# A transformer block on one core: value loads on ACT's queue, broadcasts of reciprocals on GpSimd's, first conditioning rows taken out of PSUM by ACT, and turned chunks in wide tiles

## The chip, the cores and the metric

The kernel runs on one core of a Trainium2 chip. The metric is device time in microseconds, the median over runs. A core has five engines with a queue of instructions each: PE (TensorE, matmuls into PSUM), DVE (VectorE), ACT (ScalarE), POOL (GpSimd) and SP (SyncE, which only issues transfers). Each queue is worked off in order: an instruction that waits for a semaphore holds up all behind it on its engine. A transfer (DMA) is an instruction of the queue that issues it (SP, ACT or POOL). All numbers are float32.

## The reference

One conditioned transformer block, for `x` of 2 x 2048 x 576, 16 heads of 36 channels, a hidden width of 2304:

```python
ada = silu(c) @ W_ada + b_ada                  # one row of 6 x 576 per batch entry
shift_msa, scale_msa, gate_msa, shift_mlp, scale_mlp, gate_mlp = split(ada, 6)
h = layernorm(x) * (1 + scale_msa) + shift_msa
q, k, v = heads(h @ W_qkv + b_qkv)
attn = softmax(einsum('blhd,bmhd->bhlm', q * 36 ** -0.5, k))
x = x + gate_msa * (einsum('bhlm,bmhd->blhd', attn, v) @ W_proj + b_proj)
h = layernorm(x) * (1 + scale_mlp) + shift_mlp
x = x + gate_mlp * (gelu(h @ W_fc1 + b_fc1) @ W_fc2 + b_fc2)
```

The layer norm has no parameters of its own; `gelu` is the tanh form.

## The kernel before

Every instruction of note goes through `seq` and keeps the order in which the program states it. So the order on each engine is the order of the Python code, and the tile framework adds the waits.

**The start (the `front` pools, L174 to L582).** Tokens are worked in stages of 512 (`queries_keys_values`, L207), a generator that is advanced step by step: load x; means, variances and the normed tile `xn` (DVE); turn `xn` into `hT`, channels on partitions, in five chunks of 128 channels (`turn`, L233: four transposes on PE into one PSUM bank; `modulated`, L151: scale and shift on the way out of PSUM, even chunks on DVE, odd ones on ACT); then the projections `pq` (L277) for queries and keys, and `pv` (L327) for values, which are stored to memory (`qk_d`, `v_d`). Five stages run here: the four of the first batch entry and the first of the second. PSUM has three wide tiles of two banks (`wide`, tag "w") and two single banks (`bank`, tag "b"). The first stage turns two chunks in banks, two in a wide tile and the fifth in half of another; the other stages turn all five in the two banks, one after the other. While stage n runs its projections, the next one is turned at its seventh step (L579).

Conditioning: `rows_of` (L403) multiplies the activated condition with one sixth of `W_ada` into a wide tile `pa`; DVE copies the row out. `modulation` (L423) turns this row into columns with ten small matmuls (L431), and `done` stores them in `mod`, from which `modulated` reads. Parts 0 and 1 are made before the first `hT`. The biases of queries, keys and the first MLP matrix come in as rows `b_in` and are transposed after that (L562), in a single bank. The remaining four parts are made by `later` between the steps of the stages, with the gated copies of `W_proj` and `W_fc2`.

**Attention (L587 on).** A unit is one head of one block of 512 queries; 8 blocks of 16 heads make 128 units, each of four slots (`NG`). The loop at L1320 goes through the slots; scores run eight slots ahead of their use (`AHEAD`). In each slot: scores (`scores`, L636, 16 matmul instructions, into two wide PSUM tiles), ACT copies them to SBUF (`keep`, L649), DVE keeps a running maximum (`maxima`, L654), subtracts the final maximum (`less`, L691), ACT takes the exponential (`exps`, L695), PE multiplies by the values (`weigh`, L707). In the first slot of a unit the chain of the maximum runs for the unit ahead: PE turns the running maxima (`turn`, L672), DVE reduces them (L682), SP writes them to memory (`m_d<-mx`, L683) and reads them back on all partitions (`m<-m_d`, L686).

Loads of a unit, all on SP: keys and queries (`load_keys`, L169 and L170, called at L1326), and values (`load_values`, L617, two buffers, called at L1327 in the first slot of the unit before). A unit's result `up` has one buffer: ACT copies it (L719), DVE adds the other half (L720), and one slot later SP stores its lower half (L726, L727) and POOL adds the upper half in memory (L728, L729). The sums of the exponentials are row 0 of the result.

**Beside attention** PE gets other work: the projections of the second batch entry, and for every finished block of queries `gather` and `block`. `fill` (L1304) emits one piece of it in the even slots, `advance` (L1288) one step of a generator per slot. `lights` are pieces that turn normed tiles (`turned`, L844: four transposes, L851, into a bank of `ps_f`, and ACT's `modulated`); in odd slots that aren't forced, up to two of them are emitted ahead of the scores (L1333).

`gather(k)` (L1032) loads the sums (L1035), the block's result `oT` and x; DVE takes the reciprocal (L1050), POOL writes it to `rec_d` (L1051). Then `rec_d` is read back in five steps, one chunk of 128 channels each, spread over the 36 partitions of every head: 22 transfers per block on SP (L1063) into tiles `r` that share four buffers with the normed tiles. DVE multiplies three steps later (`LAG`, L1072). `block(k)` projects (`po`, L787), adds x, norms, and runs the MLP: `pf` (L1160) from weights loaded one pair of chunks ahead (`load_cols`, L754 and L757, on POOL), `py` (L1208) from weights loaded at L1123 (POOL), and DVE's addition (`add`, L1220). After the last slot of attention the loop at L1381 runs the rest without it.

Of the kernel before, what the change touches and what calls it, by code (L numbers as in the profile page):

```python
# [17 lines left out]
P = 128  # L18
# [4 lines left out]
def dit_block_kernel(  # L23
# [16 lines left out]
    nc = tc.nc  # L40
    B, L, C = x.shape
# [3 lines left out]
    SCALE = D ** (-0.5)  # L45

    KC = (C + P - 1) // P
# [6 lines left out]
    NF = FF // P  # L54
    C2 = C // 2
# [3 lines left out]
    def seq(ins):  # L59

        return tc.keep_in_program_order(ins)
# [23 lines left out]
    ident = const.tile([P, P], F32, name="ident")  # L85
    make_identity(nc, ident)
    qscale = const.tile([P, 1], F32, name="qscale")
# [7 lines left out]
    NQK = 2 * C // P  # L95
    bias = const.tile([P, NQK + NF], F32, name="bias")
# [77 lines left out]
    with ExitStack() as front:  # L174
# [4 lines left out]
        def wide(name):  # L179
            return ps_w.tile([P, 2, 512], F32, tag="w", name=name)  # L180

        def bank(name):
            return ps_b.tile([P, 512], F32, tag="b", name=name)
# [23 lines left out]
        def queries_keys_values(b, tb):  # L207
            mvs = lnp.tile([P, TB, nc.vector.BN_AGGR_DIM], F32, tag="mv", name=f"mv_{b}_{tb}", bufs=2)
            xts, xns = [], []
            for i in range(TB):  # L210
                xt = lnp.tile([P, C], F32, tag="xt", name=f"xt_{b}_{tb}_{i}", bufs=8)
                by = nc.sync if (b, tb) == (0, 1) else nc.scalar
# [20 lines left out]
            def turn(kc, pt=None):  # L233
                if pt is None:
                    pt = bank(f"pt_{b}_{tb}_{kc}")
                for i in range(TB):
                    seq(nc.tensor.transpose(pt[:, ts(i, P)], xns[i][:, ts(kc, P)], ident))
                return pt

            pts = []  # L240
            if (b, tb) == (0, 0):
                spare = [wide(f"pt_{i}") for i in range(2)]
                pts = [turn(kc) for kc in range(2)]
                pts += [turn(2 + n, spare[0][:, n, :]) for n in range(2)]
                pts.append(turn(4, spare[1][:, 0, :]))
                pms.extend([spare[1][:, 1, :]])
                yield
            for kc in range(KC):
                pt = pts[kc] if kc < len(pts) else turn(kc)
# [102 lines left out]
        first_keys = []  # L352
        hTs = {}
        pms = []
        stages = [queries_keys_values(0, tb) for tb in range(NQB)] + [queries_keys_values(1, 0)]

        next(stages[0])
# [42 lines left out]
            seq(nc.tensor.transpose(pt[:, ts(kc, B)], c_in[:, ts(kc, P)], ident[:B, :B]))  # L400
        cT = ap.tile([P, KC, B], F32, name="cT")
        seq(nc.vector.tensor_copy(cT.rearrange("p k b -> p (k b)"), pt[:, 0 : KC * B]))
        def rows_of(part):  # L403

            wa = was.pop(part)
            pa = pas.pop(part) if part in pas else cleared(part)
            for n in range(2):
                for kc in range(KC):
                    at = 32 * (kc % NC)
                    seq(  # L410
                        nc.tensor.matmul(
                            pa[at : at + B, n, :C2],
                            lhsT=cT[: rows(kc), kc, :],
                            rhs=wa[: rows(kc), kc, ts(n, C2)],
                            start=(kc < NC),
                            stop=(kc == KC - 1 or 0 < kc < NC),
                        )
                    )
            t = ap.tile([P, C], F32, tag="rows", name=f"rows_{part}", bufs=2)
            seq(nc.vector.tensor_copy(t.rearrange("p (n c) -> p n c", n=2), pa[:, :, :C2]))  # L420
            return t

        def modulation(part, t):  # L423

            pm = pms.pop(0) if pms else wide(f"pm_{part}")[:, 0, :]
            if part == 0:
                pms.append(pm[:, KC * B :])
            for fc in range(KC):
                m = P if fc < KC - 1 else KL
                seq(  # L430
                    nc.tensor.matmul(  # L431
                        pm[:m, ts(fc, B)], lhsT=t[:, ds(fc * P, m)], rhs=of_b, start=True, stop=True
                    )
                )
            to = 2 * (part // 3) + (1 - part % 3)
            add = 1.0 if part % 3 == 1 else 0.0
            spans = [(0, P, 0, KC - 1), (0, KL, KC - 1, KC), (64, KL, KC - 1, KC)]

            def done():
                for at, m, lo, hi in spans:  # L440
                    seq(
                        nc.vector.tensor_scalar_add(
                            mod[at : at + m, to, lo:hi, :].rearrange("p k b -> p (k b)"),
                            pm[:m, lo * B : hi * B],
                            add,
                        )
                    )

            return done
# [103 lines left out]
            modulation(4, t)()  # L553

        next(stages[0])
        ts_ = [rows_of(part) for part in range(2)]
        next(stages[0])
        for done in [modulation(part, ts_[part]) for part in range(2)]:
            done()
        pt = bank("pt_bias")  # L560
        nb = NQK + NF
        seq(nc.tensor.transpose(pt[:, 0:nb], b_in, ident[:nb, :nb]))  # L562
        nq = C // P
        seq(nc.vector.tensor_scalar_mul(bias[:, 0:nq], pt[:, 0:nq], SCALE))
        seq(nc.vector.tensor_scalar_mul(bias[:, nq : nq + 1], pt[:, nq : nq + 1], qscale))
        seq(nc.vector.tensor_copy(bias[:, nq + 1 : nb], pt[:, nq + 1 : nb]))

        for b in range(B):
            seq(nc.vector.tensor_copy(spread[b], of_b[:, b : b + 1].to_broadcast([P, P])))
        rest = later()  # L570
        next(rest)
        next(stages[0])
        for n in range(NQB):
            if n + 2 <= NQB:
                next(stages[n + 2])
# [11 lines left out]
    with ExitStack() as main_part:  # L587
# [12 lines left out]
        class Unit:  # L600
# [11 lines left out]
            def load_values(self):  # L612
                self.v = np_.tile([P, L // P * HA + 64 - HA], F32, tag="v", name=f"v_{self.u}")
                nt = L // P * HA
                seq(nc.vector.memset(self.v[:, nt:], 0.0))
                seq(
                    nc.sync.dma_start(  # L617
                        out=self.v[:, :nt].rearrange("p (t e) -> p t e", e=HA),
                        in_=v_d[self.b].rearrange("(t p) e -> p t e", p=P)[
                            :, :, ds(self.h * HA, HA)  # L620
                        ],
                    )
                )
# [408 lines left out]
        def gather(k):  # L1032

            sums = bp.tile([P, H * QB // P], F32, tag="sums", name=f"sums_{k}")
            seq(nc.gpsimd.dma_start(out=sums, in_=flat_rows(sum_d[k])))  # L1035
            oT = hp.tile([P, KC, QB], F32, tag="big", name=f"oT_{k}")
            outs[k] = oT
            seq(
                nc.gpsimd.dma_start(
                    out=oT[:, 0 : KC - 1, :],  # L1040
                    in_=o_d[k][0 : (KC - 1) * P].rearrange("(kc p) n -> p kc n", p=P),
                )
            )
            for half in halves(oT, KC - 1):
                seq(nc.gpsimd.dma_start(out=half, in_=o_d[k][(KC - 1) * P : C]))
            b, qb = divmod(k, NQB)
            loaded[k] = load_x(f"b{k}", b, qb, gp_d[b])
            yield
            yield
            seq(nc.vector.reciprocal(sums, sums))  # L1050
            seq(nc.gpsimd.dma_start(out=flat_rows(rec_d[k]), in_=sums))  # L1051
            yield
            recs = []
            LAG = 3
            for kc in range(KC + LAG):
                if kc < KC:
                    r = xp.tile([P, CP], F32, tag="xn", name=f"r_{k}_{kc}")[:, :QB]
                    for to in (0,) if kc < KC - 1 else (0, 64):
                        f, end = kc * P, min(kc * P + P, C)
                        while f < end:  # L1060
                            n = min(D - f % D, end - f)
                            seq(
                                nc.sync.dma_start(  # L1063
                                    out=r[ds(to + f - kc * P, n), :],
                                    in_=rec_d[k][f // D, :].partition_broadcast(n),
                                )
                            )
                            f += n
                    recs.append(r)
                if kc >= LAG:  # L1070
                    c = kc - LAG
                    seq(nc.vector.tensor_mul(oT[:, c, :], oT[:, c, :], recs[c]))  # L1072
                yield
# [246 lines left out]
        for G in range(-AHEAD, NU * NG + 1):  # L1320
# [3 lines left out]
            su, sg = divmod(G + AHEAD, NG)  # L1324
            if sg == 0 and su + 1 < NU:
                units[su + 1].load_keys()  # L1326
            if g == 0 and -1 <= u and u + 1 < NU:  # L1327
                units[u + 1].load_values()
            cu, cg = divmod(G - 1 + AHEAD, NG)
            chain = cg == NG - 1 and 0 <= cu < NU  # L1330
            count(RATE)
            forced = g % 2 == 0 or G < 0 or credit > RATE
            if not forced:  # L1333
                for step in [lights.pop(0)() for _ in lights[:2]]:
                    count(-step[0])
                    step[1]()
            tiles = units[su].scores(sg) if su < NU else None
            if tiles:
                units[su].keep(sg, tiles)
            dones = fill() if forced else []  # L1340

            if 0 <= G + 1 < NU * NG:
# [98 lines left out]
```

## Time and profile before

| | us |
|---|---|
| median of 3 runs (lowest, highest) | 3733.76 (3732.9, 3734.05) |
| the profiled execution, outside | 3736.07 |
| its span, first to last instruction | 3734.3 |
| PE busy in the span | 3692.3 |
| DVE, ACT, POOL busy | 2947.2, 2329.2, 616.2 |
| mean clock granted to PE | 0.996 |

The profile is that of one execution. A line of the timeline gives start, length, engine, source line, operation, output<-inputs, shapes, count, and in brackets the idle time of the engine before it with what ended it; "SPq" is SP's queue, on which a transfer's length is the time of its issue. A line of the waits gives the engine and line that waited, for whom, the total in us, how often, and the longest. In the busy table by stretch the columns are busy us (and instructions) of PE, PE's weight loads, DVE, ACT and POOL, then PE's clock as a share of full speed, the mean busy share of the 16 DMA engines, and GB/s. A busy PE is not PE at its peak. Idle time of an engine that doesn't set the end costs nothing.

### The profile page before, as it was taken

What the parts mean: (1) busy time and instruction counts of PE and PEld (TensorE: products, weight loads), DVE (VectorE), ACT (ScalarE), POOL (GpSimd) and SP (SyncE); (2) the same over time, 40 slices, a digit from 0 to 9 for tenths busy, and PEclk for the clock granted to TensorE, in tenths of its full rate; (3) what the DMA queues carried; (4) which work ended last, traced back from release to release, by engine and by line L of the source; (5) the groups of instructions that cost most, each with busy time, mean ns of one, the idle gap of its engine ahead of it and who ended that gap; (6) DMA issues with size and microseconds to landing.
All of it is one profiled execution on the core that took longest, in us unless ns stands there. A gap on an engine that the chain in (4) does not pass through costs nothing. (4 is left out here: it accounts for less than half of the span.)

```text
span 3734.3 us, 59188 instructions
## 1 busy us (share of the span) xinstructions
PE 3692.3 (99%) x23926; PEld 1724.1 (46%) x23926; DVE 2947.2 (79%) x3002; ACT 2329.2 (62%) x2164; POOL 616.2 (17%) x868
## 2 busy tenths in 40 slices
PE   8999999999999999999999999999999999999999
PEld 4454344434444534444444444453444444444565
DVE  4627889889888898898889888988889888988422
ACT  0006777667776686677677767767667766676321
POOL 0101111211111111111121112111120211111311
PEclk9999999999999999999999999999999999999999
DMA  7733444554345343534353435424353435342522
GB/s 237 270 109 99 100 95 98 126 108 106 73 89 116 77 100 71 132 68 99 79 120 83 112 65 112 110 59 105 78 122 66 103 79 116 79 100 58 136 70 70
DMA packets 426864, 382.11 MB, mean 102 GB/s; under 512 B 313734, under 2 KB 314776, under 8 KB 426592
## 3 DMA queue, kind: packets, MB, share of 16 engines
q1 hardware_dynamic: 354336, 178.84, 22.5%
q0 software_dynamic: 69952, 194.77, 19.8%
q10 hardware_dynamic: 2304, 4.72, 0.4%
q8 instruction: 189, 3.10, 0.4%
q14 instruction: 83, 0.68, 0.1%
HBM read 306.98 MB, written 71.21 MB: 101 GB/s over the span
## 5 line engine op out<-in xcount | busy, mean ns | idle before, releaser
L649 ACT COPY e<-s 128x1024 f32<-128x1024 f32 x1024 | 989.5, 1024 | 716.2 <-PE s L636 714.4
L691 DVE TENSOR_TENSOR e<-e,m 128x2048 f32<-128x2048 f32 x512 | 1161.7, 2274 | 58.8 <-DMA m<-m_d 58.8
L654 DVE TENSOR_TENSOR acc<-acc,e 128x1024 f32<-128x1024 f32 x768 | 939.1, 1223 | 184.8 <-ACT e L649 142.7
L695 ACT ACTIVATE e<-e 128x2048 f32<-128x2048 f32 x512 | 990.9, 1936 | 20.7 <-DVE e L691 20.7
L707 PE MATMUL av<-e,v 64*64 64x512 f32 x8192 | 980.4, 594 | 0.0
L636 PE MATMUL s<-qT,kT 36*64 36x512 f32 x8192 | 974.0, 589 | 1.5 <-PE pv L327 1.0
L1208 PE MATMUL py<-w,gT 128*128 128x288 f32 x2304 | 585.6, 412 | 6.3 <-DVE x_b L1220 6.3
L636 PEld LDWEIGHTS s<-qT,kT 36*64 36x64 f32 x8192 | 311.0, 133 | 561.8 <-issue 520.6
L707 PEld LDWEIGHTS av<-e,v 64*64 64x64 f32 x8192 | 298.1, 133 | 518.9 <-issue 466.8
L1160 PE MATMUL pf<-h_b,w_b 128*128 128x512 f32 x1152 | 531.0, 604 | 0.0
L1208 PEld LDWEIGHTS py<-w,gT 128*128 128x128 f32 x2304 | 434.8, 191 | 184.8 <-issue 43.7
L728 POOL DMA_DIRECT2D o_d<-up x128 | 109.5, 856 | 2086.0 <-DMA o_d<-up 1277.4
L1160 PEld LDWEIGHTS pf<-h_b,w_b 128*128 128x128 f32 x1152 | 207.7, 189 | 318.8 <-issue 305.3
L1171 ACT ACTIVATE gT<-pf,bias 128x512 f32<-128x512 f32 x144 | 99.0, 688 | 191.3 <-PE pf L104 133.4
L682 DVE TENSOR_REDUCE mx<-mt 128x4 f32<-128x512 f32 x128 | 88.1, 688 | 159.8 <-PE mt L672 159.8
L1180 DVE SCALAR_TENSOR_TENSOR th<-th,gT 128x1024 f32<-128x1024 f32 x72 | 88.0, 1223 | 90.7 <-ACT th L1178 90.5
L654 DVE TENSOR_TENSOR acc<-e 128x1024 f32<-128x1024 f32 x128 | 155.4, 1214 | 4.4 <-ACT e L649 4.4
L1220 DVE TENSOR_TENSOR x_b<-py,x_b 128x288 f32<-128x288 f32 x192 | 81.0, 450 | 83.3 <-PE py L1208 83.2
L729 POOL DMA_DIRECT2D sum_d<-up x128 | 143.7, 1123 | 0.9 <-issue 0.9
L277 PE MATMUL pq<-hT,w_in 128*128 128x512 f32 (+1 forms) x320 | 131.8, 564 | 1.5 <-DVE hT L156 1.5
L787 PE MATMUL po<-wpr_p,oT 128*128 128x288 f32 x512 | 132.6, 412 | 0.0
L754 POOL DMA_DIRECT2D w_b<-in_L_cond_W_fc_dram x72 | 69.5, 965 | 303.1 <-PE pf L1160 272.6
(157 smaller groups left out, 2353.1 us busy)
## 6 DMA issues: line engine op xcount, KB each, us to landing
w<-w_d POOLq DMA_DIRECT2D x72, 576.0 KB, 6.0
v<-v_d SPq DMA_DIRECT2D x128, 296.0 KB
kT<-qk_d SPq DMA_DIRECT2D x256, 144.0 KB
w_b<-in_L_cond_W_fc_dram POOLq DMA_DIRECT2D x72, 512.0 KB, 4.8
m<-m_d SPq DMA_DIRECT2D x128, 256.0 KB
qT<-qk_d SPq DMA_DIRECT2D x256, 72.0 KB
w_d<-wg POOLq DMA_DIRECT2D x12, 864.0 KB, 6.8
qk_d<-ev SPq DMA_DIRECT2D x36, 256.0 KB
```

The source lines that it names most:

```text
L277: nc.tensor.matmul(pq[:, r, :n], lhsT=w_in[:, kc, cols], rhs=hT[:, kc, at], start=(kc == 0 and not (two and r)), stop=(kc == KC - 2 and tw ...
L636: nc.tensor.matmul(s[ts(c, 64), i, :], lhsT=self.kT[at, ds((2 * g + j) * P + 64 * c, 64)], rhs=self.qT[at, :], start=True, stop=True,)
L649: seq(nc.scalar.copy(self.es[g][:, j], s))
L654: top = lambda out, x, y: seq(nc.vector.tensor_max(out, x, y))
L691: seq(nc.vector.tensor_sub(e, e, m))
L695: seq(nc.scalar.activation(e, e, AF.Exp))
L707: nc.tensor.matmul(self.av[ts(i, 64), r, :], lhsT=self.v[ts(r, 64), ds((c + i * (HALF // P)) * HA, 64)], rhs=e[ts(r, 64), j, i, :], start= ...
L728: seq(nc.gpsimd.dma_start(out=o, in_=hi[1:HA, :], accum_op=ALU.add))
L729: seq(nc.gpsimd.dma_start(out=sums, in_=hi[0:1, :], accum_op=ALU.add))
L787: nc.tensor.matmul(outs[n][:, :C2], lhsT=src[:, kc, ts(i, P)], rhs=w_[:, kc, ts(n, C2)], start=(kc == 0), stop=False,)
L1160: nc.tensor.matmul(pfs[j], lhsT=wc[:, kc, ts(j, P)], rhs=h2[:, kc, :], start=(kc == 0 and j == 0), stop=(kc == KC - 2 and j == 1),)
L1208: nc.tensor.matmul(py[n][:, :C2], lhsT=gTs[f - f % 2][:, f % 2, ts(i, P)], rhs=w2s[f - f % 2][:, f % 2, ts(n, C2)], start=(j == 0), stop=( ...
```

## The change

Five edits:

1. `load_values` issues its transfer on ACT's queue instead of SP's, and is called in the second slot of the unit before, not the first.
2. The 22 broadcasts of reciprocals per block (`r<-rec_d`) are issued on POOL's queue instead of SP's.
3. In odd slots the `lights` come after the scores and their copies, not ahead of them.
4. The rows of conditioning parts 0 and 1 are copied out of PSUM by ACT. Their `modulation` matmuls are emitted before the transposes of the first stage, into the two halves of one wide tile, and are stored after them. The biases are transposed along with the first stage's fifth chunk, in the other half of its tile, and kept after the first `hT` has been made.
5. Every stage at the start turns its third and fourth chunk in a wide tile; before, the first stage alone did. The fifth chunk of the other stages stays in a single bank.

```diff
-            pts = []
-            if (b, tb) == (0, 0):
-                spare = [wide(f"pt_{i}") for i in range(2)]
-                pts = [turn(kc) for kc in range(2)]
-                pts += [turn(2 + n, spare[0][:, n, :]) for n in range(2)]
-                pts.append(turn(4, spare[1][:, 0, :]))
-                pms.extend([spare[1][:, 1, :]])
+            first = (b, tb) == (0, 0)
+            pts = [turn(kc) for kc in range(2)]
+            spare = wide(f"pt_{b}_{tb}")
+            pts += [turn(2 + n, spare[:, n, :]) for n in range(2)]
+            if first:
+                spare = wide("pt_4")
+                pts.append(turn(4, spare[:, 0, :]))
+                turn_biases(spare[:, 1, :])
                 yield
...
+        nb, nq = NQK + NF, C // P
+        turned_biases = []
+
+        def turn_biases(pt):
+            turned_biases.append(pt)
+            seq(nc.tensor.transpose(pt[:, 0:nb], b_in, ident[:nb, :nb]))
+
+        def keep_biases():
+            pt = turned_biases[0]
+            seq(nc.vector.tensor_scalar_mul(bias[:, 0:nq], pt[:, 0:nq], SCALE))
+            seq(nc.vector.tensor_scalar_mul(bias[:, nq : nq + 1], pt[:, nq : nq + 1], qscale))
+            seq(nc.vector.tensor_copy(bias[:, nq + 1 : nb], pt[:, nq + 1 : nb]))
...
-        def rows_of(part):
+        def rows_of(part, by=None):
...
-            seq(nc.vector.tensor_copy(t.rearrange("p (n c) -> p n c", n=2), pa[:, :, :C2]))
+            out = t.rearrange("p (n c) -> p n c", n=2)
+            if by is nc.scalar:
+                seq(nc.scalar.copy(out, pa[:, :, :C2]))
+            else:
+                seq(nc.vector.tensor_copy(out, pa[:, :, :C2]))
...
-            if part == 0:
-                pms.append(pm[:, KC * B :])
...
         next(stages[0])
-        ts_ = [rows_of(part) for part in range(2)]
+        ts_ = [rows_of(part, nc.scalar) for part in range(2)]
+        both = wide("pm")
+        pms.extend(both[:, n, :] for n in range(2))
+        dones = [modulation(part, ts_[part]) for part in range(2)]
         next(stages[0])
-        for done in [modulation(part, ts_[part]) for part in range(2)]:
+        for done in dones:
             done()
-        pt = bank("pt_bias")
-        nb = NQK + NF
-        seq(nc.tensor.transpose(pt[:, 0:nb], b_in, ident[:nb, :nb]))
-        nq = C // P
...
+        next(stages[0])
+        keep_biases()
         for b in range(B):
             seq(nc.vector.tensor_copy(spread[b], of_b[:, b : b + 1].to_broadcast([P, P])))
         rest = later()
         next(rest)
-        next(stages[0])
...
                 seq(
-                    nc.sync.dma_start(
+                    nc.scalar.dma_start(
                         out=self.v[:, :nt].rearrange("p (t e) -> p t e", e=HA),
...
                             seq(
-                                nc.sync.dma_start(
+                                nc.gpsimd.dma_start(
                                     out=r[ds(to + f - kc * P, n), :],
...
-            if g == 0 and -1 <= u and u + 1 < NU:
+            if g == 1 and -1 <= u and u + 1 < NU:
                 units[u + 1].load_values()
...
             forced = g % 2 == 0 or G < 0 or credit > RATE
+            tiles = units[su].scores(sg) if su < NU else None
+            if tiles:
+                units[su].keep(sg, tiles)
             if not forced:
                 for step in [lights.pop(0)() for _ in lights[:2]]:
                     count(-step[0])
                     step[1]()
-            tiles = units[su].scores(sg) if su < NU else None
-            if tiles:
-                units[su].keep(sg, tiles)
             dones = fill() if forced else []
```

More of the change, by code (lines that the diff above doesn't have):

```diff
@@ L555, in dit_block_kernel @@
         next(stages[0])
-        ts_ = [rows_of(part) for part in range(2)]
+        ts_ = [rows_of(part, nc.scalar) for part in range(2)]
+        both = wide("pm")
+        pms.extend(both[:, n, :] for n in range(2))
+        dones = [modulation(part, ts_[part]) for part in range(2)]
         next(stages[0])
-        for done in [modulation(part, ts_[part]) for part in range(2)]:
+        for done in dones:
             done()
-        pt = bank("pt_bias")
-        nb = NQK + NF
-        seq(nc.tensor.transpose(pt[:, 0:nb], b_in, ident[:nb, :nb]))
-        nq = C // P
-        seq(nc.vector.tensor_scalar_mul(bias[:, 0:nq], pt[:, 0:nq], SCALE))
-        seq(nc.vector.tensor_scalar_mul(bias[:, nq : nq + 1], pt[:, nq : nq + 1], qscale))
-        seq(nc.vector.tensor_copy(bias[:, nq + 1 : nb], pt[:, nq + 1 : nb]))
+        next(stages[0])
+        keep_biases()
         for b in range(B):
```

## The prediction

> **What bounds the kernel now.** I read four views: busy times, what each queue waited for, the order of time around the longest waits, and the busy table by stretch, for the clock.
>
> ```profile
> PE 3692.3 (99%) x23926; PEld 1724.1 (46%) x23926; DVE 2947.2 (79%) x3002; ACT 2329.2 (62%) x2164; POOL 616.2 (17%) x868
> ```
>
> PE is busy all but 42.0 us of the 3734.3 us span, and none of its matmuls go away. So only PE's idle time, and time at a low clock, can be won. The waits of PE (us in all, times, longest):
>
> ```profile
> PE mt L672 <- DVE acc L654: 8.7, 2, 8.0
> PE py L1208 <- DVE x_b L1220: 6.3, 2, 3.8
> PE pt L237 <- DVE hT L156: 4.0, 8, 0.6
> PE pt_b L851 <- DVE x_b L1220: 2.4, 6, 0.4
> PE pt_bias L562 <- ACT hT L154: 1.5, 1, 1.5
> PE pq L277 <- DVE hT L156: 1.5, 1, 1.5
> ```
>
> The largest are three stops in the attention part, at 766 (7.96 us), 2752 (3.75) and 3157 (2.58). All come where a block's reciprocals are fetched. In SP's own waits one line stands out:
>
> ```profile
> SPq L1063 <- DMA rec_d<-sums: 234.7, 8, 30.9
> ```
>
> Some 29 us per block, SP stands at the first broadcast of reciprocals (L1063) until GpSimd has written them to memory. Everything later in SP's order stands behind it, in order of time (start, length):
>
> ```profile
> 2728.71 0.69 DVE L682 TENSOR_REDUCE mx<-mt 128x4 f32<-128x512 f32 x1 [0.74 <-PE mt L672]
> ...
> 2732.17 0.91 POOL L1051 DMA_DIRECT2D rec_d<-sums  x1
> ...
> 2737.96 1.48 SPq L1063 DMA_DIRECT2D r<-rec_d  x4
> ...
> 2741.15 0.39 SPq L617 DMA_DIRECT2D v<-v_d  x1
> ...
> 2741.95 1.88 SPq L683 DMA_DIRECT2D m_d<-mx  x1
> ...
> 2746.67 0.32 SPq L686 DMA_DIRECT2D m<-m_d  x1
> ...
> 2749.80 2.29 DVE L691 TENSOR_TENSOR e<-e,m 128x2048 f32<-128x2048 f32 x1 [11.04 <-DMA m<-m_d]
> ...
> 2752.51 8.54 PE L1208 MATMUL py<-w,gT 128*128 128x288 f32 x24 [3.75 <-DVE x_b L1220]
> ```
>
> The maxima are ready at 2729.4, yet leave only at 2741.95. DVE stands 11.04 us at the subtraction, behind it stands the addition that would free PSUM, and PE stops. The 24 matmuls that follow take 8.54 us; the same group undisturbed took 6.09 (at 2735.64). The clock is the reason, as the busy table by stretch shows (last three columns: clock, DMA share, GB/s):
>
> ```profile
> 25.00:26.00 1.00, 1.00 (x2) 0.34 (x1) 1.00 (x3) 0.78 (x1) 0.00 (x0) 0.50 1.07 391
> 3156.00:3157.00 1.00, 0.00 (x0) 0.00 (x0) 1.00 (x1) 0.00 (x0) 1.00 (x2) 0.93 0.53 186
> 3158.00:3159.00 1.00, 1.00 (x3) 0.71 (x3) 1.00 (x2) 1.00 (x1) 0.00 (x0) 0.50 0.73 168
> ```
>
> The start has the same fault:
>
> ```profile
> 17.01 1.41 DVE L420 COPY rows<-pa 128x576 f32<-128x576 f32 x2
> 18.84 2.35 PE L431 MATMUL pt<-of_b,rows 128*128 128x2 f32 x20
> 22.72 0.24 PE L562 MATMUL pt_bias<-ident,b_in 27*128 27x27 f32 x1 [1.53 <-ACT hT L154]
> 24.41 6.58 PE L277 MATMUL pq<-hT,w_in 128*128 128x512 f32 x8 [1.46 <-DVE hT L156]
> ```
>
> PE stops at 21.19, projections start at 24.41, eight matmuls take 6.58 us where the next sixteen take 7.13 (31.95). The clock is at half until about 30.2.
>
> **The change, part by part.**
>
> **Reciprocals on GpSimd's queue (L1063), values on ACT's (L617).** SP loses 22 issues per block with their wait, and one per unit. Then m_d leaves at 2729.4 and needs about 1.4 us to m's issue (2762.85 to 2764.29 in an undisturbed unit) and 3.1 us to the subtraction (2746.67 to 2749.80): 2734, where DVE comes to it at 2738.75. The 11 us go, and the three stops with them. Idle: 7.96 + 3.75 + 2.58 = 14.3 us. Clock: half speed costs half of the busy time in it, 766.29 to 770.94 2.3 us; 8.54 - 6.09 = 2.5; 9.07 - 6.09 = 3.0; 7.8 together. **-22.1 us.** Here a rule and the row differ. The Trainium skill (TensorE: Matmul & The Clock Gate, "Why this matters for your kernels") calls gaps up to about 3 us harmless. The row at 3158 shows 0.50 after 2.58 us. By the rule this part is worth 19.1 us, by the row 22.1; I take the row.
>
> A rule that speaks against this part: the skill (DMA: Bandwidth & Descriptors, "Specifications" and "Issuing engines are not separate DMA queues") gives GpSimd's path 1 us to the first byte against 0.6, and says that another issuing engine saves only issue time. By that alone: 22 x 0.36 us of issue per block off SP, none of it on PE's path, no gain, and 22 x 0.4 = 8.8 us later data per block. The trace shows instead what in-order waiting costs. And lateness has cover: the multiplication is three steps behind its broadcast (LAG), and a step of work takes some 6 us (724 to 747: four). GpSimd's queue then carries, per block, the wait for rec_d (5.8 us to landing) and 22 issues. It has no broadcast this small; nearest is x_b<-gp_d, four in 2.23 us, 0.55 each: 12 us. It stands in front of weight loads and of the o_d and sum_d additions (L728), for which ACT's copy of the next unit's result waits (one buffer). Weights are loaded one pair of chunks ahead, about 19 us here, against 5 us of landing; the additions have three slots of some 6 us. Bounds: 0, to 18 us less those 14 of slack, 4 per block, 28 for the seven blocks fetched beside attention. I take **0**. In the stretch after attention PE runs up to 3543 before it needs the product: last r issues end at 3538.8 now. With 18 of them from 3526.2 at 0.55, three w loads at 0.7 and the last four, they end at 3540.5; the quarter matmuls that need the last chunk come at 3547.31. 0.
>
> ACT issues 128 value loads, 0.39 us on SP, 0.45 on ACT at the start (four in 1.81): 58 us. The work that hides it is ACT's own wait for scores, 714.4 us before L649, 5.7 at a time after a filled slot. Behind the load stand the copies and the next exponential. The buffer's last reader (L707 of the unit before) comes ahead of scores that ACT has copied already, so no wait is added. One slot later leaves three slots, about 17 us, for a load of 2048 packets (by queue q1's 22.5% over 354336 packets, 38 ns a packet on 16 engines: 5 us). **0**; uncovered it is 58.
>
> **Rows on ACT, modulation before the turns, biases turned with them.** pa is done at 15.96. ACT copies 128x576 in about 0.64 (L719's 512 takes 0.58, L649's 1024 1.02): 16.75. Twenty L431 matmuls end at about 18.3, then 20 transposes at 0.122 and the biases (0.24): 21.0. Meanwhile DVE stores mod (0.79) from 18.5 and hT's first chunk (0.8) by 20.1; ACT does the second. Projections start at 21.0 rather than 24.41: 3.4 us. PE has no gap near 2 us (the clock fell 1.8 to 2.5 us into each of the four), so they run at full speed: 6.58 - 3.45 = 3.1. Against: PE comes to the conditioning part 2 at 37.2 rather than 43.66. DMA is saturated: up to that load 11.8 MB are asked for, the rates sum to 9.6 MB by 30 us and 3.3 in the next 10, so it lands near 38, 0.9 us of wait. Bounds 0 to 7 (no gain); I take **-5.6**.
>
> **Chunks 2 and 3 in a wide tile**, for four later turns. The waits for hT (4.0 us, eight) go. But it takes one of three wide buffers. If these come round in order, the gate's second tile (69.5) and the last projection tile at 194.8 get the buffer of the tile just finished. Evacuation takes 0.2 + 1.41 (L265 at 194.80), so waits of 0.6 and 1.6 us arise. -4.0 to -1.8; I take **-1.8**.
>
> **Light steps after the scores.** L851's waits in odd slots (2.4 for x_b, 0.8 for h_b, 0.2) are passed while PE does 1.8 us of scores. ACT's h_b comes 1.9 us later, and its bank is next wanted after 3.6 us of other matmuls: 0. **-3.3**, at least 0.
>
> Sum: 22.1 + 5.6 + 1.8 + 3.3 = 32.8 us of the profiled 3734.3. That execution took 3736.07 outside in, 2.3 more than the median of the runs; taken off the median: 3733.8 - 32.8 = **3701 us**.
>
> **Rivals.** *GpSimd's queue takes over SP's wait:* something useful is queued behind the 18 us. For: its waits at L728 for o_d are long, 1277 us. Against: PE never waits for a weight. Half of the 22 us gone: 3712. *The start doesn't move* (weights or conditioning late, or buffers short): the DMA share of 1.05 speaks for it, that w_in's first third is asked for at 9.5 speaks against. 3701 + 7 = 3708. *The maxima stay late* because something else stands ahead on SP (kT, qT wait 1276.8 us for PE): only the other parts, 3734 - 11 = 3723. Against: in ordinary units m_d follows mx within 0.1 us. *Slower:* ACT's issue at the head of slot 1 is on the path. Place: between an exponential and the next copies. Price 0.45 x 128 = 58 us, 3759 in full. It decides from 0.26 us per unit (32.8 / 128). Against: the 5.7 us of idle after those copies; for: DVE waits 147 us for these copies, 146 times.
>
> **How the numbers follow.** Likeliest 0.50 (own range 3695 to 3707: the start's and the wide tiles' bounds), GpSimd 0.15, start 0.16, maxima 0.08, slower 0.09, other 0.02. A measurement here tells about 0.2% (7.5 us) from no change. Below 3726: 0.87; within 0.04; slower 0.09. The range 3694 to 3717 holds the first three and leaves out the maxima, the slower case and the tails.
>
> **What would show it.** DVE's wait for m under 10 us in all (58.8 now); no PE wait above 1 us after 300 us; clock 1.00 at 25 and 3158; projections at about 21; new waits of pq or pg for ev if the wide buffers are short; GpSimd's L1063 waiting for rec_d near 6 us a block. Wrong if PE waits for w_b, w_q or v, or if ACT's copies become what PE's scores wait for.

## Result and profile after

The changed kernel takes **3704.88 us** (median of 5 runs, 3702.62 to 3712.05); in the same comparison the kernel before takes 3733.76 (3729.91 to 3735.7). The ratio is **0.9924, 95% interval 0.9913 to 0.9934**: 28.4 us less (0.0076 x 3734). Predicted were 3701, with 3694 to 3717 around it. The profiled execution of the changed kernel took 3707.24 us with a span of 3705.5, against 3736.07 and 3734.3: 28.8 us less, where the prediction's sum had 32.8.

The page's busy line, in the form of the one before:

```profile
PE 3682.3 (99%) x23926; PEld 1722.0 (46%) x23926; DVE 2948.0 (80%) x3000; ACT 2327.3 (63%) x2166; POOL 706.2 (19%) x1044
```

PE is idle for 23.2 us now (3705.5 - 3682.3), where it was idle for 42.0, and busy for 10.0 us less with the same 23926 matmuls: most of that is time at half clock that is gone. The waits of PE of 1 us and more (us in all, times, longest):

```profile
PE pa L425 <- DMA wa<-in_L_cond_W_ada_dram: 7.8, 2, 4.6
PE pt_c L414 <- ACT c_in L411: 4.9, 1, 4.9
PE mt L684 <- DVE acc L666: 3.0, 3, 1.9
PE mt L684 <- ACT e L661: 1.9, 3, 0.8
PE s L648 <- DVE mx L694: 1.1, 1, 1.1
PE s L648 <- PE pv L328: 1.0, 1, 1.0
```

The stops of 7.96, 3.75 and 2.58 us are gone, and so are the waits for `hT`, for the turned biases and in front of the `lights`. One thing is new on the list: `pa` waits twice for conditioning weights (7.8 us, where it waited once, 4.1). Small waits at `mt` and `s` are left. The queues (GpSimd's wait at the broadcasts, DVE's for `m` and for `r`):

```profile
POOL r L1075 <- DMA rec_d<-sums: 57.3, 8, 8.6
```
```profile
DVE oT L1084 <- DMA r<-rec_d: 31.2, 9, 8.4
```
```profile
L703 DVE TENSOR_TENSOR e<-e,m 128x2048 f32<-128x2048 f32 x512 | 1162.8, 2276 | 9.8 <-DMA m<-m_d 9.8
```

SP's 234.7 us at the broadcasts have become 57.3 on GpSimd, 7.2 per block. DVE's wait for `m` fell from 58.8 to 9.8. Its wait for `r` rose from 17.0 to 31.2. The site shown before (2729 to 2752) now reads, in order of time:

```profile
2710.85 0.68 DVE L694 TENSOR_REDUCE mx<-mt 128x4 f32<-128x512 f32 x1
...
2711.56 0.34 SPq L695 DMA_DIRECT2D m_d<-mx  x1
...
2722.72 2.29 DVE L703 TENSOR_TENSOR e<-e,m 128x2048 f32<-128x2048 f32 x1 [1.99 <-DMA m<-m_d]
...
2725.01 2.06 POOL L1075 DMA_DIRECT2D r<-rec_d  x4 [7.29 <-DMA rec_d<-sums]
...
2730.89 0.69 DVE L1084 TENSOR_TENSOR oT<-oT,r 128x512 f32<-128x512 f32 x1 [5.14 <-DMA r<-rec_d]
...
2737.12 0.72 PE L684 MATMUL mt<-ident,acc 128*128 128x128 f32 x4 [1.93 <-DVE acc L666]
2737.77 3.45 PE L719 MATMUL av<-e,v 64*64 64x512 f32 x16
```
```profile
2738.00:2739.00 1.00, 1.00 (x8) 0.27 (x4) 1.00 (x2) 0.00 (x0) 0.26 (x1) 0.53 0.56 154
```

The maxima leave 0.03 us after they are reduced; before it was 12.5 us. But DVE then stands 5.14 us at the multiplication by `r`, the running maximum behind it comes late, and PE still stops for 1.93 us. The four transposes after this stop run at full clock; from about 2738.1 the clock is at half for 3.4 us, and the 16 matmuls behind the transposes take 3.45 us where such a group takes 1.90 to 1.95 elsewhere. The start:

```profile
16.39 2.45 PE L447 MATMUL pm<-of_b,rows 128*128 128x2 f32 x20
18.77 2.40 PE L237 MATMUL pt<-ident,xn 128*128 128x128 f32 x20
21.10 0.24 PE L361 MATMUL pt<-ident,b_in 27*128 27x27 f32 x1
21.27 3.70 PE L278 MATMUL pq<-hT,w_in 128*128 128x512 f32 x8
...
40.81 3.66 PE L425 MATMUL pa<-wa,cT 128*2 128x288 f32 x20 [3.11 <-DMA wa<-in_L_cond_W_ada_dram]
```
```profile
25.00:26.00 1.00, 1.00 (x9) 0.19 (x9) 0.97 (x4) 0.00 (x0) 0.00 (x0) 1.00 1.07 395
...
41.00:42.00 1.00, 1.00 (x16) 0.24 (x9) 0.00 (x0) 0.00 (x0) 0.00 (x0) 0.77 1.07 394
42.00:43.00 1.00, 1.00 (x10) 0.25 (x2) 0.00 (x0) 0.00 (x0) 0.00 (x0) 0.50 1.06 280
```

Projections start at 21.27 instead of 24.41 and at full clock (third number from the right: 1.00 at 25). Then PE stands 3.11 us for the weights of conditioning part 2, and the clock falls to half after that stop instead.

Cut at three marks of the two traces (the first `pq`, the `pa` of part 5 at 60.37 and 59.33, the first `s` of attention at 276.41 and 269.65), the 28.8 us fall like this: 3.1 gained up to the first `pq`, 2.1 lost again from there to part 5, 5.7 gained up to attention, 22.0 in attention and behind it (the stop at 2737 and its half clock included). The prediction had 5.6 in the first two together, 1.8 in the third and 25.4 in the last.

### The profile page after: what moved, and what is told of

It is laid out like the page before. It is cut to its first block, busy times and chain, and to the rows that moved or that the text cites. A ratio compares the mean times of both kernels' runs of the same rounds, so it can differ in the third digit from the quotient of the medians.

```text
span 3705.5 us, 59239 instructions
## 1 busy us (share of the span) xinstructions
PE 3682.3 (99%) x23926; PEld 1722.0 (46%) x23926; DVE 2948.0 (80%) x3000; ACT 2327.3 (63%) x2166; POOL 706.2 (19%) x1044
## 3 DMA queue, kind: packets, MB, share of 16 engines
q1 hardware_dynamic: 82928, 129.54, 12.5%
## 4 chain that ended last, share of the span: by engine, by line
PE 94%; DMA 3%; DVE 1%; ACT 1%; issue 1%; POOL 0%; SPq 0%; DVEq 0%; ACTq 0%; POOLq 0%
PE av L719 23%; PE s L648 22%; PE py L1220 15%; PE pf L1172 14%; PE po L799 4%; PE pq_q L975 3%; PE pq L278 3%; PE pf L104 2%; PE pv L328 2%; PE pv_q L799 2%; PE mt L684 2%; DMA x_b<-gp_d 1%; PE po L104 1%; DMA wa<-in_L_cond_W_ada_dram 1%; DVE acc L666 0%
## 5 line engine op out<-in xcount | busy, mean ns | idle before, releaser
L661 ACT COPY e<-s 128x1024 f32<-128x1024 f32 x1024 | 990.2, 1025 | 813.3 <-PE s L648 802.7
```

What stands on the lines that cost most here:

```text
L661: seq(nc.scalar.copy(self.es[g][:, j], s))
```

## Experiments

Times are compared through ratios to the kernel before, taken on the same chip; 0.001 is 3.7 us. Spans and waits are those of one profiled execution of each kernel.

**One edit of the five at a time, on the kernel before.** First the broadcasts alone:

```diff
-                                nc.sync.dma_start(
+                                nc.gpsimd.dma_start(
                                     out=r[ds(to + f - kc * P, n), :],
```

> The kernel before with the 22 broadcasts of reciprocals per block on GpSimd's queue, and nothing else changed. Theory (SP's in-order wait for rec_d is what made the maxima late): the three stops at 766, 2752 and 3157 us go almost wholly, DVE's wait for m falls from 58.8 us to under 15, time 3712 to 3715 (-19 to -22 us). Rival (the value load ahead of m_d on SP is as much to blame): the stops shrink by half, 3722 or so. Rival (GpSimd's queue takes the wait over): PE waits for weights or ACT for the result's buffer, 3725 or more.

Measured: 3720.24 us, ratio 0.9960 (0.9947 to 0.9974), 14.9 us less; span 3720.1. DVE's wait for `m` fell to 13.8 us, under 15 as expected. PE's stops at 2752 and 3157 are gone; of the one at 766 two are left (order of time, PE):

```profile
760.58 0.75 PE L672 MATMUL mt<-ident,acc 128*128 128x128 f32 x4 [2.60 <-ACT e L649]
...
767.07 1.99 PE L636 MATMUL s<-qT,kT 36*64 36x512 f32 x8 [3.01 <-DVE mx L682]
```

So this edit is most of the gain, though less than was expected of it, and the time lies nearest the rival's.

**The value loads alone:**

```diff
-            if g == 0 and -1 <= u and u + 1 < NU:
+            if g == 1 and -1 <= u and u + 1 < NU:
                 units[u + 1].load_values()
...
-                    nc.sync.dma_start(
+                    nc.scalar.dma_start(
                         out=self.v[:, :nt].rearrange("p (t e) -> p t e", e=HA),
```

> The kernel before with the value loads on ACT's queue, one slot later, and nothing else changed. Theory: SP still stands at the first broadcast for some 29 us per block, the maxima stay late, DVE's wait for m stays above 40 us, and 128 issues of 0.4 us on ACT cost nothing: 3730 to 3734. Rival (ACT is on the path): slower, up to 3790. Rival (the value load was the larger hold on SP): 3720 or less.

Measured: **3770.69 us, ratio 1.0097 (1.0083 to 1.0110): 36 us slower.** The recorded sum had 0 for this edit. ACT's waits, then the order of time around one of its stops:

```profile
ACT e L649 <- DMA r<-rec_d: 83.2, 7, 15.7
```
```profile
746.43 1.53 SPq L1063 DMA_DIRECT2D r<-rec_d  x4
...
751.35 0.37 ACTq L617 DMA_DIRECT2D v<-v_d  x1
751.81 1.93 ACT L649 COPY e<-s 128x1024 f32<-128x1024 f32 x2 [15.66 <-DMA r<-rec_d]
...
752.87 3.69 PE L636 MATMUL s<-qT,kT 36*64 36x512 f32 x16 [10.05 <-ACT e L649]
```

The maxima do stay late, as expected (DVE has reduced them by 737.75, `m_d` is issued at 751.95). But DVE's wait for `m`, expected above 40 us, is 16.2: DVE now stands for ACT's copies instead (198.1 us, where it was 147.2), and PE has seven stops for them, 35.4 us in all.

ACT's copy has nothing to do with `r`; what stands is the value load ahead of it on ACT's queue. It, too, uses no `r`. The built program says why it waits. Every transfer issued on SP or ACT signals one of eight completion semaphores, taken in turn over both queues in the order of the program, and each is held until the transfer eight before it has landed and signalled the same one. SP's order at this place, and then ACT's:

```
234 L1063 DMACopy r_0_4897<-rec_d_88 36x512 [waits ... DMAHW3_49 ...]
235 L1063 DMACopy r_0_4897<-rec_d_88 36x512 [waits DMAHW4_49]
236 L1063 DMACopy r_0_4897<-rec_d_88 36x512 [waits DMAHW5_49]
237 L1063 DMACopy r_0_4897<-rec_d_88 20x512 [waits DMAHW6_49]
238 L169 DMACopy kT_4902<-qk_d_60 36x1024 [waits PE_49]
239 L170 DMACopy qT_4903<-qk_d_60 36x512 [waits DMAHW0_49]
240 L169 DMACopy kT_4902<-qk_d_60 36x1024 [waits DMAHW1_49]
241 L170 DMACopy qT_4903<-qk_d_60 36x512 [waits DMAHW2_49]

374 L617 DMACopy v_4977<-v_d_62 128x16x37 [waits DMAHW5_49,DMAHW3_49]
```

The value load is the ninth of this row. It waits for semaphore 3, that of the first broadcast (5 is that of the load two units earlier into the same buffer). That broadcast waits for `rec_d`. GpSimd's transfers use a set of their own (DMASW), so with the broadcasts there the value load waits for no `r`. By this the two edits aren't independent, which the next run tests.

**Both queues, nothing else.**

> The reciprocals' broadcasts on GpSimd's queue and the value loads on ACT's, together, nothing else. Theory A (the two are worth what the prediction's sum gave them, because a value load on ACT waits for a broadcast only as long as that broadcast is issued on SP): 22.1 us less than the kernel before, about 3712 us; ACT waits for no r, and PE for ACT's copies under 3 us in all. Theory B (each edit keeps the effect it had alone, -14 and +36): about 3756 us, with ACT's waits of 10 to 16 us at the head of a block still there.

Measured: 3717.9 us, ratio 0.9957 (0.9943 to 0.9971), 16 us less; span 3716.1, 18.2 less. ACT waits for no `r`. Adding the two effects (3756) is refuted; theory A's direction holds, its 22.1 us do not. Two smaller stops remain:

```profile
760.32 0.75 PE L672 MATMUL mt<-ident,acc 128*128 128x128 f32 x4 [2.10 <-ACT e L649]
...
2747.33 0.72 PE L672 MATMUL mt<-ident,acc 128*128 128x128 f32 x4 [1.84 <-DVE acc L654]
```

22.1 - 2.10 - 1.84 = 18.2: the span's difference. The clock is 1.00 in each of the 7 us behind both stops, so in this execution the half clock is gone in full, and what was missed is these 3.9 us. Ahead of the second one, DVE stands 5.61 us for `r` at 2741.10.

**The broadcasts on ACT's queue** (kernel before, `nc.scalar.dma_start` for `r`, nothing else):

> The kernel before with the reciprocals' broadcasts on ACT's queue, value loads still on SP's, nothing else. Theory (a queue that stands at rec_d passes its wait to whatever is behind it in its order; on ACT that is the copies that free the scores' PSUM): ACT stands at least the 7 to 8 us per block that GpSimd stood, 8 blocks, seven of them beside attention, and PE stops for a part of it, so slower than before by 10 to 60 us, 3745 to 3795 us, with PE's scores waiting for ACT's copies, as in the run with the value loads alone. Rival (only SP is sensitive, because m_d stands there): like the run on GpSimd's queue, about 3720 us.

Measured: **3803.98 us, ratio 1.0181 (1.0167 to 1.0195): 68 us slower.** The direction is the theory's, the size beyond its 60. That only SP is sensitive is refuted. PE's waits and two of the seven stops:

```profile
PE mt L672 <- ACT e L649: 77.8, 10, 15.1
```
```profile
748.83 1.13 PE L672 MATMUL mt<-ident,acc 128*128 128x128 f32 x4 [13.38 <-ACT e L649]
...
3208.36 1.13 PE L672 MATMUL mt<-ident,acc 128*128 128x128 f32 x4 [15.10 <-ACT e L649]
```

The expectation took GpSimd's 7 to 8 us per block for ACT's. GpSimd comes to the broadcasts right after it has issued `rec_d` itself and waits for the landing alone; ACT comes to them before `rec_d` is even issued (at the first block it stands 16.36 us up to 747.76, so from 731.40 on, while `rec_d` is issued at 739.16). How long a queue stands depends on when it arrives.

**The start alone** (edit 4: rows by ACT, modulation first, biases turned along):

> The kernel before with the start's edit alone (rows of parts 0 and 1 copied by ACT, modulation ahead of the turns, biases turned along with them). The prediction on record gives it -5.6 us: 3728. After the result, the profile of the changed kernel shows projections starting 3.1 us earlier at full clock, but PE then standing 3.1 us for the weights of conditioning part 2 with the clock halved after it: by that, -1 us, 3732 to 3734.

Measured: 3731.45 us, ratio 0.9992 (0.9983 to 1.0000). Attention starts at 274.36 instead of 276.41, 2.1 us earlier. Six traces with the old start have this mark between 275.00 and 276.70, so the gain is 0.6 to 2.3 us, and by the traces the recorded 5.6 is too much; the ratio alone (0 to 6.3 us) would allow it. PE waits for the weights of part 2 here as well.

**The wide tiles alone** (edit 5):

```diff
             pts = []
             if (b, tb) == (0, 0):
...
+            else:
+                pts = [turn(kc) for kc in range(2)]
+                spare = wide(f"pt_{b}_{tb}")
+                pts += [turn(2 + n, spare[:, n, :]) for n in range(2)]
```

> The kernel before with chunks 2 and 3 of the four later turns in a wide tile, and nothing else changed. The prediction on record gives -1.8 us (two new waits where three wide buffers come round in order): 3732, with waits of pg and pq for evacuations of 0.6 and 1.6 us. Rival, from the profile of the changed kernel (no such waits; each turn 1.45 us shorter): -5.8 us, 3728.

Measured: 3728.09 us, ratio 0.9981 (0.9972 to 0.9990), 7 us less (3.7 to 10.5); attention starts at 270.84, 5.6 us earlier. The rival (5.8) is right, the recorded 1.8 too little. One turn before, and with the edit (order of time, PE):

```profile
62.41 1.09 PE L237 MATMUL pt<-ident,xn 128*128 128x128 f32 x8
64.05 1.09 PE L237 MATMUL pt<-ident,xn 128*128 128x128 f32 x8 [0.55 <-DVE hT L156]
65.61 0.66 PE L237 MATMUL pt<-ident,xn 128*128 128x128 f32 x4 [0.47 <-DVE hT L156]
66.10 3.60 PE L277 MATMUL pq<-hT,w_in 128*128 128x512 f32 x8
```
```profile
62.55 2.40 PE L237 MATMUL pt<-ident,xn 128*128 128x128 f32 x20
64.79 3.60 PE L281 MATMUL pq<-hT,w_in 128*128 128x512 f32 x8
```

3.69 us from turn to projection become 2.24, 1.45 less; the two gaps are 1.02 of it, the rest lies in three short groups becoming one. Four turns: 5.8. No wait of `pq` or `pg` for `ev` appears.

**The light steps alone** (edit 3):

> The light steps after the scores, nothing else. By the prediction's sum: 3.3 us less, about 3731 us, and PE's waits at pt_b (L851, 2.4 us in odd slots) gone. Rival: ACT takes the chunk up later and the pair of scores behind it waits; then no gain, 3734 us, with a wait of s or pt_b for ACT in its place.

Measured: 3731.7 us, ratio 0.9991 (0.9982 to 1.0); span 3731.0, 3.3 less, and no wait at `pt_b` is left in PE's list. The times by themselves don't tell it from no change. The missing wait is as expected; of the span's 3.3 us, 1.4 lie ahead of attention (its first `s` is at 275.00), where this edit changes nothing, so attention itself gave 1.9.

**More work on ACT,** behind each value load of the changed kernel:

```diff
                 units[u + 1].load_values()
+                for _ in range(3):
+                    seq(nc.scalar.copy(pad[:, 0:16], pad[:, 16:32]))
```

> The changed kernel with three more ACT copies of 128x16 behind each value load, 384 in all; by the shortest copies of ACT in the trace some 0.2 us each, 70 to 80 us of ACT time in all, more than the 58 us that the value loads' issue was put at. Theory (ACT's wait for scores covers it): within 3 us of the changed kernel, 3702 to 3708 us, ACT's wait for scores shorter by about what was added. Rival (ACT's time at the head of slot 1 is on the path): 3705 + 75 = 3780 us, and PE's scores wait for ACT's copies.

Measured: 3705.68 us, ratio 0.9920 (0.9907 to 0.9934), against 0.9924 without the copies. ACT's groups (busy us, mean ns, then its idle time and what ended it):

```profile
L661 ACT COPY e<-s 128x1024 f32<-128x1024 f32 x1024 | 990.4, 1025 | 741.4 <-PE s L648 741.4
...
L1344 ACT COPY pad<-pad 128x16 f32<-128x16 f32 x384 | 79.1, 206 | 8.1
```

79.1 us of copies cost nothing that the runs resolve (the interval is 5 us to either side), and ACT's wait for scores falls from 802.7 to 741.4. The cover that the prediction named for the 128 value loads is real. What it doesn't cover is a value load that *waits* there.

**Value loads back on SP** (edit 1 undone in the changed kernel):

> The changed kernel with the value loads back on SP's queue, a slot earlier, as before; all else as changed. Theory (once the broadcasts are off SP, the queue of the value loads is worth next to nothing: both edits gave -16 to -17 us where the broadcasts alone gave -14.4): 3704 to 3708 us, and DVE's wait for m stays under 15 us. Rival (the value loads on ACT carry a good part of the gain): 3711 us or more.

Measured: 3708.67 us, ratio 0.9929 (0.9916 to 0.9941). The interval lies over that of the changed kernel (0.9913 to 0.9934), so this edit's own part isn't resolved: 1.9 us by the ratios here, 1.1 between the two runs with the broadcasts on GpSimd (0.9960 and 0.9957). The traces of both lean the same way, with stops of 2.6 to 3.0 us that are shorter or absent with the value loads on ACT. DVE's wait for `m` stays at 12.9 us, under the 15 expected.

**Conditioning weights earlier** (changed kernel):

```diff
-        load_in(2)
-        seq(nc.sync.dma_start(out=bv, in_=b_qkv[2 * C :].partition_broadcast(P)))
...
         rest = later()
         next(rest)
+        load_in(2)
+        seq(nc.sync.dma_start(out=bv, in_=b_qkv[2 * C :].partition_broadcast(P)))
```

> The changed kernel, with the conditioning weights of parts 2 and 5 asked for ahead of the last third of w_in and of the values' bias. Theory: the wait of 3.11 us at part 2 (40.81) goes and with it the half clock after it (44.9 - 41.7 = 3.2 us at half, 1.6 to 1.9 us): about 4.9 us less than the changed kernel, 3700 us. Rival 1: the value projections then wait for their weights and nothing is won, 3705 us, with a wait of pv for w_in. Rival 2: DMA is the bound at the start whatever the order, and the wait goes to another part, 3703 to 3707 us.

Measured: 3703.91 us, ratio 0.9916 (0.9903 to 0.9930); the interval lies over the changed kernel's, so it isn't shown to be faster. In the trace the wait at part 2 is gone and the values wait for nothing:

```profile
35.37 3.70 PE L278 MATMUL pq<-hT,w_in 128*128 128x512 f32 x8
39.00 2.11 PE L423 MATMUL pa<-wa,cT 128*2 128x288 f32 x20
41.03 3.70 PE L278 MATMUL pq<-hT,w_in 128*128 128x512 f32 x8
```

Attention starts at 266.03 instead of 269.65 (267.44 in the earliest trace of that start). Rival 1 (`pv` waits) and rival 2 (the wait goes to another part) are not in the trace. This is the lowest median and the lowest ratio of all, by 1 us and by 0.0004, which is too little to claim.

## Why the prediction was right

The total came out 4 us off because, of three parts that were each missed by some 4 us, two gave less than recorded and one gave more. So the mechanisms are shown, but that the total came this near is in part luck. With the spans of the single-edit runs the parts are:

| part | recorded | shown |
|---|---|---|
| both queues | -22.1 | -18.2 (span) |
| start | -5.6 | -2.1 (first `s`, alone), -1.0 in the changed kernel up to part 5 |
| wide tiles | -1.8 | -5.6 (first `s`) |
| light steps | -3.3 | -3.3 (span; 1.9 of it in attention) |
| sum | -32.8 | -29.2, with 28.8 between the two kernels |

**Queues.** The mechanism was right: SP stood at the broadcasts, `m_d` behind them, and PE's three stops hung on that. The step that failed is "The 11 us go, and the three stops with them", with the 0 that was taken for GpSimd's queue. Two stops remained, 2.10 and 1.84 us. One is traced to the cover that was named, that the multiplication runs three steps behind its broadcast: DVE stands there 5.14 us (2730.89), in the single-edit run 5.61, and its wait for `r` rose by 14.2 us in all. The other stop (2.10, ACT's copies) comes at the same place in the first block fetched beside attention. There the run with the broadcasts alone shows:

```profile
747.09 2.07 POOL L1063 DMA_DIRECT2D r<-rec_d  x4 [8.29 <-DMA rec_d<-sums]
...
751.49 1.24 POOL L729 DMA_DIRECT2D sum_d<-up  x1
...
759.02 0.58 ACT L719 COPY up<-av 128x512 f32<-128x512 f32 x1 [4.95 <-DMA sum_d<-up]
```

The additions to `o_d` and `sum_d` stand on GpSimd's queue behind the broadcasts, ACT's copy of the next unit's result waits for them (one buffer), and the copies of the scores stand behind it; with both queues changed ACT stands 4.60 us at this copy. That is the other thing the prediction named and took at 0. Both are read from traces; no run takes the additions out of the way. So GpSimd's queue does take over a piece of SP's wait, as that rival said, but at most a fifth of the gain (3.9 of 22.1) and not half.

The 7.8 us of half clock went in full in the run with both queues. The row that the prediction took (0.50 after a stop of 2.58 us) and the changed kernel's own row (0.53 after one of 1.93 us) both speak against the Trainium skill's rule (TensorE: Matmul & The Clock Gate, "Why this matters for your kernels"), by which gaps up to about 3 us are harmless. In the changed kernel that stop brought back 3.4 us at half clock, about 1.7 us of time.

**The value load at 0** is right for the change as a whole and wrong for the edit by itself. The prediction asked whether ACT's issue time fits under its wait for scores, and 79.1 us of copies show that it does. It didn't ask what the load itself would wait for once it is counted in one turn with SP's transfers. The "slower" rival, with its price of issue time, was the wrong mechanism; the real one costs 36 us and is switched off by edit 2.

**Start.** The step that failed is "it lands near 38, 0.9 us of wait". PE was ready at 37.7, about as forecast, and the weights let it go at 40.81, a wait of 3.11 us (40.25 in the run with the extra copies, whose start is the same code). DMA's share is 1.00 to 1.13 in every microsecond from 10 to 45 of the changed kernel, so these weights came through engines that were never free. The forecast counted 11.8 MB up to this load; by 40.8 the engines had moved 13.0 (318 GB/s over 40.8 us), part of it asked for after these weights. The rival that the start doesn't move named weights being late, and gave it 7 us: 4.6 of 5.6 were in fact lost in the profiled execution, and asking for these weights earlier removes the wait.

**Wide tiles.** The waits of `pg` and `pq` for a buffer rested on an "if these come round in order". They don't appear. The upper end, 4.0, was short as well, since it counted gaps between groups and not the groups' own filling.

**What would show it:** `m` under 10 us (9.8), clock 1.00 at 25 and 3158, projections at about 21 (21.27), no waits for `w_b`, `w_q` or `v` held; GpSimd's wait near 6 us a block was 7.2; "no PE wait above 1 us after 300 us" failed at 1.93 and 1.07.

## What to carry to other kernels

Before a transfer moves to another queue, ask what the transfer itself will wait for there, its completion slot included, and not only whether the issue fits: here the same 128 loads cost nothing or 36 us, depending on where *another* transfer was issued. A wait that must stand in some queue belongs where little that is urgent stands behind it and where the queue arrives latest (GpSimd 15 us less than before, ACT 68 us more). When PE is made to start earlier, the loads that it reaches next must be asked for earlier too.

## What the runs showed of the hardware

The clock did not answer the same gap in the same way. The start of the changed kernel is the same code in three runs, with gaps at part 2 of 3.11, 2.60 and 1.48 us; only the first was followed by half clock. In attention a gap of 2.10 us (both queues) and one of 2.60 (broadcasts alone) left the transposes behind them at 0.75 us, while 2.58 before the change and 1.93 in the changed kernel were followed by half clock. Nor did the clock fall at a fixed point: the prediction read 1.8 to 2.5 us into the stop, but in the changed kernel it fell 0.7 and 0.9 us after the two stops had ended (at 41.5 and 2738.1). And with value loads back on SP the clock fell where PE had been busy since 14.17 (the last gap was 0.40 us, the one before it 4.74), in the middle of the first turn, and was back some 3.4 us later:

```profile
19.00:20.00 1.00, 1.00 (x10) 1.00 (x10) 0.93 (x7) 0.01 (x1) 0.00 (x0) 0.99 1.05 359
20.00:21.00 1.00, 1.00 (x7) 1.00 (x6) 0.60 (x1) 0.77 (x1) 0.00 (x0) 0.50 1.08 399
21.00:22.00 1.00, 1.00 (x7) 0.97 (x5) 0.45 (x1) 0.00 (x0) 0.00 (x0) 0.50 1.10 355
```

This set the scale of what single executions can show here: the first `s` of the same start code lies at 269.65, 268.06 and 267.44 us. Why the clock fell there is open. Just ahead of it lie 20 matmuls of two columns each (16.48 to 18.93), as in the runs whose clock stayed full there; whether they bear on it, no run shows.
